# The joint stages between the scans of a state-space network: how outputs and inputs are handed out, and three buffers for the tiles of the outputs

## The chip, the cores and the metric

The kernel runs on one core of one Trainium2 chip. The metric is the device time of one execution in microseconds, as the median of the runs shown. The profile is that of one execution of the same kernel.

## The reference

A batch of four images of 64 x 64 pixels with 96 channels goes through four residual layers. Layers 0 and 1 are state-space blocks, layers 2 and 3 are an attention without softmax and a feed-forward layer with rounded operands. What matters here are the first two layers. Cut to its steps, with shapes left out, one of them is:

```
x   = x + block(groupnorm(x))               # 32 groups of 3 channels, over the whole image
block(x):
  xz      = x @ in_proj_w.T                 # 96 -> 2 * 192 channels: xp and the gate z
  xc      = silu(depthwise_conv3x3(xp))
  for four directions k (rows, columns, both reversed):
      dt, B, C = split(x_proj[k] @ xc_k)    # 6 + 16 + 16 rows
      delta    = softplus(dt_proj[k] @ dt + bias)
      h[l]     = exp(delta[l] * A) * h[l-1] + delta[l] * u[l] * B[l]    # 16 states a channel
      y_k[l]   = sum over states of h[l] * C[l], + D * u[l]
  y       = sum of the four y_k, each turned back to rows
  y       = layernorm(y) * silu(z)          # over the 192 channels of a pixel
  return y @ out_proj_w.T                   # 192 -> 96 channels
```

The recurrence over the 4096 pixels of an image is the scan.

## The kernel before, in words

**Units.** A pair of images is worked on together, so each of the two state-space layers has two units, and there are four units in all: layer 0 pair 0, layer 0 pair 1, layer 1 pair 0, layer 1 pair 1. Each unit has three steps. `scan_inputs` (L157) makes the inputs of the scan: it normalises and projects the image (`xn`, `ips`), writes the gate to HBM (`zs` to `zg`), and computes the convolution, in part as nine matmuls with diagonal weights (`conv_product`, L189, `cps`) and in part as chains of nine VectorE instructions (`conv_chain`, L203 and L205, into `u`). At its end it begins the projection and discretisation for the first piece of the scan (`scan.begin`: `xps`, `btps`, `bpps`, `dps`, `delta`, `du`, and the transposes `dups` with their copies `dut`, L478 and L480). `PairScan.scan` runs the scan itself. `scan_outputs` (L272) makes the outputs from the sums `y`, which the scan has stored in HBM.

**The outputs.** `scan_outputs` takes 256 pixels of both images at a time, 16 groups in all. A group loads the gate (`zt`, L285), the residual (`xr`, L287) and the sums (`ys`, three loads on L296); VectorE takes the statistics (`ystats`, `ymv`); POOL takes a power for the reciprocal deviation (`ln_rs`, L81); ScalarE normalises `ys` (L311); TensorE turns it in six transposes (`pt`, L319), ScalarE scales these into `gt` (L321), VectorE multiplies `gt` with `zt` (L328), TensorE projects (`po`, L335 in layer 0; L345, L346 and L348 in layer 1), and the sum with the residual (`xo`) is stored. In layer 0 VectorE also takes the statistics for the group norm of the next layer, and after the sixteenth group the norm is finished (`mv`, `gm`, `gv`, L123 to L138). These tiles live in the pool `c2`, which has two buffers of each, and three in the last unit.

**Stages.** The program has nine stretches in a row: inputs of unit 0; scan 0; joint stage; scan 1; joint stage; scan 2; joint stage; scan 3; and the token layers, which contain the outputs of unit 3. In a joint stage the outputs of the unit that has just been scanned and the inputs of the next unit are traced together. Both are generators. `scan_outputs` yields after every group, so 16 times; `scan_inputs` yields 20 times (eight projections of each image, a yield after every second, then six rounds of two yields). `between_scans` (L142) takes one group of the outputs and then two pieces of the inputs, in turn, so that the inputs are used up after ten groups.

**What sets the order.** Outside the scans the order of each engine is not that of the program text alone: a scheduler places each instruction on its engine's list when its operands and a buffer are there by its own estimate, with the order of tracing as priority. Within the scan every instruction is kept in program order. On the chip each engine then takes its list strictly in order. All loads and stores are issued by one queue, SP, also in order. The pools of a joint stage (inputs `a`, `a2`, `a_ps`; outputs `c2`, `c_ps`) are given back when both generators are done, and the scan's pools take that memory.

Of the kernel before, what the change touches and what calls it, by code (L numbers as in the profile page):

```python
# [141 lines left out]
def between_scans(tc, cst, ident, half, pn, u, before, scan, after):  # L142


    with ExitStack() as stage:
        ins = scan_inputs(tc, stage, cst, ident, half, pn, u, scan, *after)
        if before is not None:
            pp = stage.enter_context(tc.tile_pool(name="c_ps", bufs=2, space=PSUM))
            outs = scan_outputs(tc, stage, cst, ident, half, pn, *before, pp)
            for _ in outs:  # L150
                for _ in range(2):
                    next(ins, None)
        for _ in ins:
            pass
# [117 lines left out]
def scan_outputs(tc, stage, cst, ident, half, pn, layer, pr, pp, turned="pt", summed="po"):  # L272

    nc = tc.nc
    par, zg, x_src, x_dst, y = layer.par, layer.zg[pr], layer.x_src, layer.x_dst, layer.y[pr]
    p2 = stage.enter_context(tc.tile_pool(name="c2", bufs=3 if layer.last and pr else 2))
    if not layer.last:
        norms = [GroupNorm(p2, pn, f"gn{2 * pr + i}", NT // 2) for i in range(2)]
    wo = p2.tile([128, 3, C], F32, name="wo", bufs=1)
# [2 lines left out]
    for g in range(NT // 2):  # L282
# [46 lines left out]
        bufs = 1 if summed == "po" else None  # L329
# [559 lines left out]
def token_layers(tc, cst, ident, half, x, outputs, a):  # L889
# [3 lines left out]
    with ExitStack() as stage:  # L893
# [28 lines left out]


        outs = scan_outputs(tc, stage, cst, ident, half, None, *outputs, pp, "mm", "o")
        images = [image(b) for b in range(NB)]
        begun, going, turns = 0, [], 0
# [13 lines left out]
def hybrid_kernel(ctx: ExitStack, tc: tile.TileContext, a):  # L940
# [14 lines left out]
    with ExitStack() as scans:  # L955
        pw = scans.enter_context(tc.tile_pool(name="s_w", bufs=1))
        pn = scans.enter_context(tc.tile_pool(name="s_n", bufs=1))
        units = []
        for n in range(2):
            layer = ScanLayer(tc, pw, dram, x, {k: a[f"l{n}_{k}"] for k in ("par", "wi", "wx", "wdt", "wo")}, n)  # L960
            units += [(layer, pr) for pr in range(NB // 2)]
            x = layer.x_dst
        units[0][0].after = units[2][0]
        with ExitStack() as scanning:
            pk = scanning.enter_context(tc.tile_pool(name="s_k", bufs=2))
            pu = scanning.enter_context(tc.tile_pool(name="s_u", bufs=1))
            pq = scanning.enter_context(tc.tile_pool(name="s_q", bufs=1))
            pd = scanning.enter_context(tc.tile_pool(name="s_d", bufs=2, space=DRAM))
            cst["sel"] = pu.tile([NP, NS, 256], BF16, name="sel")
            nc.sync.dma_start(out=cst["sel"], in_=a["c_sel"])  # L970
            cst["ident16"] = pu.tile([128, 128], BF16, name="ident16")
            nc.vector.tensor_copy(cst["ident16"], ident)
            u = [pu.tile([128, L], F32, name=f"u{j}") for j in range(3)]
            before = None
            for unit in units:
                scan = PairScan(tc, pk, pq, pd, cst, ident, u, *unit)
                between_scans(tc, cst, ident, half, pn, u, before, scan, unit)
                scan.run()
                before = unit
        token_layers(tc, cst, ident, half, x, before, a)  # L980
# [113 lines left out]
```

## Time and profile before

| | us |
|---|---|
| median of 3 runs (10634.33 to 10654.25) | 10643.59 |
| the profiled execution | 10644.94 |
| its span, first to last instruction | 10643.2 |
| inputs of unit 0, up to the first `bp` of scan 0 | 0 to 154.9 |
| first joint stage, end of the last `ysum` to the first `bp` | 2461.7 to 2678.6 |
| second joint stage | 4984.3 to 5197.6 |
| third joint stage | 7500.1 to 7713.7 |
| token layers with the outputs of unit 3 | 10014.9 to 10643.2 |

In the profile PE is TensorE's matmul and PEld its weight load, DVE is VectorE, ACT ScalarE, POOL GpSimd and SP the engine that issues the transfers. A slice of the page is one fortieth of the span, 266 us, and a digit is the busy share in tenths. In a list of groups the columns are line, engine, operation and tile, shapes, count, busy time, mean duration in ns, and the idle time just before with what ended it. A matmul of float32 operands shows as two records.

### The profile page before, as it was taken

What the parts mean: (1) busy time and instruction counts of PE and PEld (TensorE: products, weight loads), DVE (VectorE), ACT (ScalarE), POOL (GpSimd) and SP (SyncE); (2) the same over time, 40 slices, a digit from 0 to 9 for tenths busy, and PEclk for the clock granted to TensorE, in tenths of its full rate; (3) what the DMA queues carried; (4) which work ended last, traced back from release to release, by engine and by line L of the source; (5) the groups of instructions that cost most, each with busy time, mean ns of one, the idle gap of its engine ahead of it and who ended that gap; (6) DMA issues with size and microseconds to landing.
All of it is one profiled execution on the core that took longest, in us unless ns stands there. A gap on an engine that the chain in (4) does not pass through costs nothing. (4 is left out here: it accounts for less than half of the span.)

```text
span 10643.2 us, 142480 instructions
## 1 busy us (share of the span) xinstructions
PE 8055.8 (76%) x47648; PEld 5971.9 (56%) x47648; DVE 9608.1 (90%) x6922; ACT 8760.2 (82%) x18779; POOL 9008.7 (85%) x5298
## 2 busy tenths in 40 slices
PE   7777777777777777777877777777777777777666
PEld 4555555554555555555455555555455555555554
DVE  8999999997899999998899999999699999999755
ACT  6888888885888888887688888888598888888666
POOL 3999999993899999997499999999299999999745
PEclk9888899988888898988888988998888889899877
DMA  4677777775667777777467777777566777777710
GB/s 154 208 211 215 216 222 218 219 213 158 196 210 216 217 220 220 219 214 210 149 209 211 220 219 218 220 219 217 143 209 211 213 220 219 220 217 219 199 35 25
DMA packets 905175, 2120.41 MB, mean 199 GB/s; under 512 B 330583, under 2 KB 640153, under 8 KB 706713
## 3 DMA queue, kind: packets, MB, share of 16 engines
q1 hardware_dynamic: 904440, 2111.30, 68.3%
q8 instruction: 378, 6.19, 0.2%
q14 instruction: 357, 2.92, 0.1%
HBM read 1949.56 MB, written 161.48 MB: 198 GB/s over the span
## 5 line engine op out<-in xcount | busy, mean ns | idle before, releaser
L71 POOL TENSOR_TENSOR h<-h,cb 128x1024 f32<-128x1024 f32 x3072 | 7191.2, 2364 | 234.4 <-issue 58.6
L71 DVE TENSOR_TENSOR_SCAN h<-da,last,bp 128x1024 f32<-128x1024 f32 x2064 | 4736.8, 2335 | 147.1 <-PE bp L71 23.8
L71 ACT ACTIVATE x<-dut,bt 128x128 f32<-128x128 f32 x12288 | 3494.8, 370 | 1.5 <-PE bp L71 1.1
L71 PE MATMUL yp<-ident,h 128*128 128x128 f32 x24576 | 3370.2, 297 | 9.8 <-POOL h L71 9.8
L71 PEld LDWEIGHTS yp<-ident,h 128*128 128x128 f32 x24576 | 3197.1, 157 | 125.7 <-issue 75.5
L71 ACT ACTIVATE da<-delta,amat 128x1024 f32<-128x1024 f32 x2752 | 3060.2, 1138 | 96.0 <-DVE h L71 94.9
L71 PE MATMUL bp<-ident,x 128*128 128x128 f32 x10240 | 1679.2, 316 | 1282.1 <-DVE h L71 923.7
L71 PEld LDWEIGHTS bp<-ident,x 128*128 128x128 f32 x10240 | 1362.6, 162 | 1840.7 <-ACT x L71 1026.7
L71 DVE TENSOR_TENSOR bp<-du,bp 128x1024 f32<-128x1024 f32 x1472 | 1780.1, 1213 | 266.0 <-PE bp L71 264.4
L71 DVE TENSOR_TENSOR_SCAN h<-da,bp 128x1024 f32<-128x1024 f32 x688 | 1537.7, 2274 | 52.7 <-ACT da L71 11.4
L71 PE MATMUL bp<-bparts,sel 96*128 96x512 bf16 x2944 | 918.8, 398 | 760.4 <-DVE h L71 741.2
L71 PEld LDWEIGHTS <-sel 96*128 96x128 bf16 x2944 | 226.8, 100 | 1554.8 <-DVE h L71 1043.7
L71 ACT ACTIVATE bp<-delta,amat 128x1024 f32<-128x1024 f32 x320 | 358.1, 1119 | 528.3 <-DVE h L71 526.3
L71 POOL TENSOR_TENSOR dbu<-du,bb 128x1024 f32<-128x1024 f32 x320 | 754.6, 2358 | 0.0
L71 DVE TENSOR_TENSOR_SCAN h<-bp,last,dbu 128x1024 f32<-128x1024 f32 x240 | 558.9, 2329 | 10.4 <-POOL dbu L71 7.1
L81 POOL TENSOR_TENSOR ln_rs<-ln_ve,half 128x4 f32<-128x4 f32 x64 | 82.4, 1288 | 567.2 <-DVE ln_ve L79 442.0
L71 PE MATMUL xps<-u,wx 128*76 128x512 f32 x720 | 532.0, 824 | 0.0
L71 ACT ACT_TABLE_LOAD x380 | 487.5, 1283 | 34.6 <-DVE gn_norm L138 22.4
L71 POOL COPY last<-h 128x2 f32<-128x2 f32 x1152 | 215.8, 187 | 351.0 <-DVE h L71 349.1
L71 POOL TENSOR_TENSOR du<-delta,u 128x1024 f32<-128x1024 f32 x188 | 496.2, 2639 | 0.0
L71 ACT COPY ysum<-yp 128x1024 f32<-128x1024 f32 x192 | 194.4, 1012 | 300.3 <-PE yp L71 300.3
L71 PE MATMUL dps<-cdt,wdt 12*128 12x512 f32 x752 | 435.0, 658 | 0.0
(159 smaller groups left out, 6328.0 us busy)
## 6 DMA issues: line engine op xcount, KB each, us to landing
cb<-crow SPq DMA_DIRECT2D x1024, 1024.0 KB
cb<-crow SPq DMA_DIRECT2D x1024, 512.0 KB
bb<-crow SPq DMA_DIRECT2D x384, 256.0 KB
bb<-crow SPq DMA_DIRECT2D x128, 512.0 KB
y<-ysum SPq DMA_DIRECT2D x192, 256.0 KB
kept<-y SPq DMA_DIRECT2D x160, 256.0 KB
y<-ysum SPq DMA_DIRECT2D x64, 512.0 KB
zt<-zg SPq DMA_DIRECT2D x64, 384.0 KB
```

Of the source, the lines that this page charges most:

```text
L71: return self.tc.keep_in_program_order(getattr(self.engine, op)(*args, **kwargs))
L81: nc.gpsimd.tensor_tensor(rs, ve, half, ALU.pow)
```

## The change

Two lines differ. In `between_scans` the outputs are counted, and after a group one piece of the inputs is taken, after every fourth group two, so that 20 pieces go to 16 groups: five pieces for four groups. In `scan_outputs` the pool `c2` has three buffers of each tile in every unit.

```diff
@@ between_scans @@
             outs = scan_outputs(tc, stage, cst, ident, half, pn, *before, pp)
-            for _ in outs:
-                for _ in range(2):
+            for g, _ in enumerate(outs):
+                for _ in range(2 if g % 4 == 3 else 1):
                     next(ins, None)
         for _ in ins:
             pass
@@ scan_outputs @@
-    p2 = stage.enter_context(tc.tile_pool(name="c2", bufs=3 if layer.last and pr else 2))
+    p2 = stage.enter_context(tc.tile_pool(name="c2", bufs=3))
```

## The prediction

> **What bounds the kernel now.** I read the page's busy rows and slices first, then the busy time by window around the places where the slices dip, then groups, waits and the order of time inside one dip.
>
> ```profile
> PE 8055.8 (76%) x47648; PEld 5971.9 (56%) x47648; DVE 9608.1 (90%) x6922; ACT 8760.2 (82%) x18779; POOL 9008.7 (85%) x5298
> ...
> DVE  8999999997899999998899999999699999999755
> ...
> POOL 3999999993899999997499999999299999999745
> ```
>
> Over the span DVE and POOL are the full engines, but the slices show two regimes. The four scans run DVE and POOL at 9; POOL falls to 2 to 4 between them, in the three joint stages. The change touches no instruction of a scan, so the 90% of DVE says nothing on it: only the dips count. Each dip by windows, cut at three places: from the end of the last sum of a scan to PE's first work, to the end of the last instruction of the inputs (the copy of `dut`, L480), to the first `bp` matmul of the next scan (columns: stretch and length, busy time and count of PE, weight loads, DVE, ACT and POOL, granted clock, DMA share, GB/s).
>
> ```profile
> 2461.70:2476.80 15.10, 0.00 (x0) 0.00 (x0) 2.66 (x12) 0.58 (x3) 7.51 (x22) 0.59 0.82 190
> 2476.80:2632.10 155.30, 144.03 (x426) 70.01 (x426) 130.39 (x240) 95.08 (x181) 17.27 (x11) 0.97 0.48 140
> 2632.10:2678.60 46.50, 28.48 (x86) 17.73 (x87) 23.11 (x77) 17.47 (x40) 4.57 (x5) 0.68 0.38 110
> 4984.30:4999.30 15.00, 0.73 (x3) 0.47 (x3) 3.27 (x13) 1.33 (x4) 7.51 (x22) 0.59 0.83 206
> 4999.30:5153.60 154.30, 143.34 (x425) 69.59 (x423) 129.62 (x238) 94.44 (x180) 17.27 (x11) 0.97 0.47 139
> 5153.60:5197.60 44.00, 26.33 (x86) 16.36 (x87) 23.20 (x77) 17.50 (x40) 4.57 (x5) 0.74 0.40 117
> 7500.10:7515.00 14.90, 0.00 (x0) 0.00 (x0) 2.52 (x12) 0.47 (x2) 7.52 (x22) 0.59 0.83 198
> 7515.00:7667.80 152.80, 146.28 (x546) 77.41 (x546) 118.11 (x210) 99.56 (x192) 16.58 (x11) 0.98 0.48 141
> 7667.80:7713.70 45.90, 31.20 (x150) 27.14 (x151) 13.04 (x46) 19.82 (x46) 4.03 (x4) 0.63 0.37 108
> ```
>
> The joint stages last 216.9, 213.3 and 213.6 us. In their middle PE is busy 93% (144.0/155.3), 93% and 96%: PE bounds it, with DVE at 84, 84 and 77%. In the tails, 46.5 + 44.0 + 45.9 = 136.4 us together, no engine is over 68%: six groups of outputs are left over and run alone, one waiting for the other:
>
> ```profile
> POOL ln_rs L81 <- DVE ln_ve L79: 21.1, 3, 10.9
> ...
> DVE xo L337 <- PE po L335: 13.1, 5, 3.7
> PEld po L335 <- DVE gt L328: 10.3, 4, 2.8
> ...
> ACT ys L311 <- DVE shift L307: 9.8, 4, 3.9
> ```
>
> These waits of the first tail run in a ring: DVE waits for PE, PE for DVE, ACT for DVE. That the next scan waits for the ring's end is seen in order of time:
>
> ```profile
> 2673.02 0.68 DVE L337 TENSOR_TENSOR xo<-xr,po 96x512 f32<-96x512 f32 x1 [3.74 <-PE po L335]
> ...
> 2674.41 1.01 DVE L123 BATCH_NORM_AGGREGATE mv<-gn_stats 96x2 f32<-96x96 f32 x2
> ...
> 2678.62 1.01 PE L71 MATMUL bp<-bparts,sel 96*128 96x512 bf16 x2 [0.24 <-DVE gn_ve L79]
> ```
>
> The pools of the scan take the memory that the stage's pools give back, so its first `bp` comes only when outputs, norms and inputs are all done. The tail is on the path of the whole kernel.
>
> **What the Trainium skill says.** "Perfetto Trace Analysis", Optimization Strategy: where the most-contended engine changes over time, interleaving the regimes can help, and the same gap repeating may mean too few buffers. The windows agree with the first half (PE at 93%, then 61%); the second fits the tail, whose groups come every 6 to 8 us with two buffers. "TensorE: Matmul & The Clock Gate", What's actually happening: the array falls to half clock after an idle window and returns after about 3.4 us of sustained work. The trace agrees in direction: granted clock 0.97 in the first middle and 0.68 in its tail, and `po` matmuls of 396 ns mean against 611. "ScalarE: Activation LUTs", What ACT_TABLE_LOAD costs: about 1283 ns a load; the trace's 380 loads have a mean of 1283. The built program has as many loads after the change as before, so I price them at nothing; ACT is busy only 61% of the middle, which would hide a few.
>
> **The change part by part.** No computing instruction is added or removed. In the order of the built program the scans, the first stage and the last one stand as before; in each joint stage the number of `po` groups behind the last transposes of the inputs (`dups`, L478) falls from six to none.
>
> *Six groups into the middle, by PE.* Warm, ten `po` groups take 20.2 us (80 records), 2.02 each, and 66 `pt` transposes, eleven groups, 11.5 us, 1.05 each. The first tail holds six groups of `po` and five of `pt`: 6 x 2.02 + 5 x 1.05 = 17.4 us of warm PE time (cold, the tail's rows show 20.9 + 6.9 us). The second is alike. For the third, the middle has 146.3 us of PE for the same ten groups against 144.0, so 0.23 more a group: 18.8 us. If PE stays at the share of each middle, and 1.9 us of it (one product of the inputs, below) moves ahead:
> first (144.0 + 17.4 - 1.9)/0.927 = 172.0, 16.7 longer than 155.3;
> second (143.3 + 17.4 - 1.9)/0.929 = 170.9, 16.6 longer;
> third (146.3 + 18.8 - 1.9)/0.957 = 170.5, 17.7 longer.
>
> *The same by DVE.* The first tail's 23.1 us less some 2.2 for the group norms make 20.9; with 130.4 that is 151.3 us, at the middle's 84% 180.2, so 24.9 longer. Second: (129.6 + 21.0)/0.84 = 179.3, 25.0 longer. Third, without norms: (118.1 + 13.0)/0.773 = 169.6, 16.8 longer, so PE's 17.7 decides there.
>
> *What still stands behind.* In the first two stages the norms, 5.6 us from the `xo` of 2673.02 to `bp`; some conv matmuls and `dups` now stand between the last `po` and the norms' matmuls, so 5 behind PE's end (bounds 4 and 8). The third has no norms: 2 us for the copies of `dut` and `xo` (bounds 1 and 4).
>
> *Sum.* By PE: (46.5 - 16.7 - 5) + (44.0 - 16.6 - 5) + (45.9 - 17.7 - 2) = 24.8 + 22.4 + 26.2 = 73 us. By DVE: 16.6 + 14.0 + 26.2 = 57 us. Both engines cannot wait less for each other while both do more, so I take the slower reading rounded, **58 us**.
>
> *Third buffer.* It adds a third set of `zt`, `xr`, `ys`, `gt` and `xo` (13 KB a partition). With 16 groups in some 172 us, 11 us apart, loads are early anyway; in the first middle DVE waited 2.6 us for `ys`. I take 0; bounds are 0 and 2.6 us a stage. Its price is on SP: a third group's five loads, at about 0.4 us of issue each 2 us, now come before the stage's fourth `xn`. PE's first products use the three `xn` loaded earlier, which hides them; uncovered, it is 2 us a stage.
>
> *`xn` loads.* In the built program the first three move ahead of the store of the last `ysum` on SP, and the first product ahead of the first `pt`: hence the 1.9 us (two cold `ips` records at 2477.97 take 1.92). These loads wait for a DVE and an ACT instruction; the last scan on DVE ended at 2456.9, before SP needs to store `ysum` at 2461.7, so I charge nothing. Queued behind them are two weight loads and that store, for which the outputs wait. Bounds: 3 us gained a stage, 3 lost.
>
> **Rivals.** *(a) In-order stalls, slower.* PE and DVE take their work in a fixed order, so a `pt` or `po` that isn't ready holds back the conv matmuls behind it. In the first middle this cost PE about 8.5 us for ten groups (7.4 for `gt`, 1.1 for `ys` after the lead-in), 0.85 a group. The gain of the PE reading, 24.8 us over 16 groups, is gone at 1.5 us more a group, 2.4 in all; the tail itself shows 9.1 + 3.3 = 12.4 us over six, 2.1. At 3.0 a stage loses 16 x 0.65 = 10 us: 10674 us. Against it: in the new order other matmuls stand between a group's `pt` and its `po`, as in the middle of before. *(b) Only the buffer works.* If the merged middle stretches by all that the tail gives, but groups then come as in the last stage, which has three buffers already (16 groups in 10066 to 10155, 5.9 us each) instead of 6.6, 6.2 and 7.6, then 5 x (0.7 + 0.2 + 1.7) = 13 us: 10630. *(c) The start of the scan is late for another reason,* since `delta`, `du` and `dups` of the inputs now share engines with outputs: six groups' DVE time, 21 us, put before `du` would leave 46 - 21 - 5 = 20 us a stage, 10584, which is my forecast again. *(d) That outputs and inputs don't end together* is ruled out by the built order.
>
> **How the numbers follow.** The profiled execution took 10644.9 us (span 10643.2 and 1.7 around it), 1.3 above the median of 10643.6; I count from the median: 10643.6 - 58 = **10586 us**. Chances: absorbed in the middle 0.85 (own range 10562 to 10612: the PE reading and 10 more, down to 32); (b) or most of the gain eaten 0.10; (a) 0.05. A measurement of this kernel tells about 0.2%, 21 us, from no change. Of the first case I put nearly all beyond that: faster 0.86, same 0.09, slower 0.05. The range, 10560 to 10628, adds the bounds of the start and the norms and part of (b).
>
> **What would show it.** The stages should be 190 to 202 us long, no `po` should come after `dups`, POOL's dip should be narrower, and the granted clock should stay above 0.9 up to the norms. PE's wait for `gt` and `ys` over 25 us a stage would mean (a); a middle stretched to 195 us with DVE under 80% too. A changed length of a scan would be outside all of this, and prove the whole sum wrong.

## The result, and the profile after

| | before | after |
|---|---|---|
| median of 6 runs each, us | 10644.94 (10634.33 to 10654.25) | 10595.13 (10584.92 to 10607.82) |
| the profiled execution | 10644.94 | 10593.83 |
| joint stages (end of the last `ysum` to the first `bp`) | 216.9, 213.3, 213.6 | 197.2, 200.1, 195.1 |
| sum of the three | 643.8 | 592.4 |

The ratio of after to before is 0.9954, with a 95% interval of 0.9943 to 0.9966: 49.8 us less by the medians, where 58 were forecast. The three stages give 19.7, 13.2 and 18.5 us, 51.4 together, close to the 51.1 us by which the two profiled executions differ. So the gain is that of these stages; the rest of the program cancels to within half a microsecond.

The page after, the busy engines and two rows of slices:

```profile
PE 8027.2 (76%) x47648; PEld 5946.6 (56%) x47648; DVE 9610.8 (91%) x6922; ACT 8761.4 (83%) x18779; POOL 9023.9 (85%) x5298
...
DVE  8999999998999999998899999999799999999755
...
POOL 3999999993999999997599999999399999999645
```

The busy sums are those of before to within 29 us (PE has 28.6 less, 16 of them in the joint stages); the instructions are as many. DVE's dips between the scans have gone from 7, 8 and 6 to 8, 8 and 7, POOL's from 3, 4 and 2 to 3, 5 and 3. The slices can show no more than that: one is 265 us, longer than a stage.

The windows after, cut at the same events: PE's first work, the end of the copy of `dut`, the first `bp` (columns: stretch and length, busy time and count of PE, weight loads, DVE, ACT and POOL, granted clock, DMA share, GB/s). In the third stage `bp` comes 0.1 us after that copy, so there is no third window:

```profile
2454.80:2469.00 14.20, 0.00 (x0) 0.00 (x0) 1.84 (x9) 0.00 (x0) 7.16 (x22) 0.50 0.79 180
2469.00:2649.90 180.90, 164.31 (x507) 83.02 (x507) 151.15 (x309) 112.95 (x221) 25.31 (x16) 0.95 0.51 147
2649.90:2652.00 2.10, 0.78 (x7) 0.61 (x8) 0.96 (x7) 0.00 (x0) 0.55 (x2) 1.00 0.00 0
4955.60:4970.00 14.40, 1.43 (x2) 0.50 (x2) 1.94 (x10) 0.29 (x2) 7.54 (x22) 0.50 0.83 194
4970.00:5153.60 183.60, 167.11 (x506) 83.59 (x505) 151.14 (x308) 112.82 (x221) 25.23 (x15) 0.93 0.50 143
5153.60:5155.70 2.10, 0.78 (x7) 0.61 (x8) 0.95 (x7) 0.00 (x0) 0.55 (x1) 1.00 0.00 0
7462.40:7477.00 14.60, 0.14 (x1) 0.14 (x1) 2.75 (x12) 0.74 (x2) 7.54 (x22) 0.50 0.83 197
7477.00:7657.40 180.40, 169.72 (x696) 95.68 (x697) 129.96 (x256) 119.14 (x236) 20.39 (x15) 0.95 0.54 149
```

The tails of 44.0 to 46.5 us at a clock of 0.63 to 0.74 are gone. The middles are 25 to 30 us longer, at a clock of 0.93 to 0.95, and PE's share of them is 91, 91 and 94%. The share of a whole middle hides what happens in it. Two pieces of the first stage:

```profile
2569.00:2589.00 20.00, 18.07 (x48) 8.52 (x47) 19.88 (x26) 4.99 (x8) 0.00 (x0) 0.91 0.17 46
2629.00:2652.00 23.00, 20.98 (x78) 11.25 (x77) 9.88 (x25) 10.88 (x20) 0.55 (x2) 1.00 0.12 32
```

Half way, DVE is full (19.9 of 20 us). At the end PE is (21.0 of 23), and DVE is at 9.9. The bound passes from one to the other inside the stage.

PE's waits in the first middle (line that waits, line waited for, us, times, longest):

```profile
PE ips L227 <- DMA zt<-zg: 15.3, 1, 15.3
PE po L335 <- DVE gt L328: 7.0, 6, 1.9
PE ips L227 <- DVE ymv L304: 4.7, 1, 4.7
PE ips L227 <- ACT ys L311: 2.6, 1, 2.6
PE pt L319 <- ACT ys L311: 1.3, 2, 1.1
```

The first of them is the lead-in. For sixteen groups PE waits 7.0 us for `gt` and 1.3 for `ys`, against 7.4 and 1.1 for ten groups before. The `po` are spread, and a gate is ready when its turn comes. The order of time at the stage's end:

```profile
2644.78 0.68 DVE L337 TENSOR_TENSOR xo<-xr,po 96x512 f32<-96x512 f32 x1 [1.34 <-PE po L335]
...
2648.01 1.04 PE L478 MATMUL dups<-ident,du 128*128 128x128 f32 x8
...
2651.98 0.61 PE L71 MATMUL bp<-bparts,sel 96*128 96x512 bf16 x2 [0.25 <-DVE gn_ve L79]
```

The last `xo` stands ahead of the inputs' last transposes (`dups`). The norms (DVE's 0.96 us in the window of 2.10) end this stage and the second; in the third `bp` waits for the copy of `dut`.

### The profile page after: what moved, and what is told of

The parts are those of the page before. It is cut to its first block, busy times and chain, and to the rows that moved or that the text cites. A ratio compares the mean times of both kernels' runs of the same rounds, so it can differ in the third digit from the quotient of the medians.

```text
span 10592.1 us, 142441 instructions
## 1 busy us (share of the span) xinstructions
PE 8027.2 (76%) x47648; PEld 5946.6 (56%) x47648; DVE 9610.8 (91%) x6922; ACT 8761.4 (83%) x18779; POOL 9023.9 (85%) x5298
## 5 line engine op out<-in xcount | busy, mean ns | idle before, releaser
L71 DVE TENSOR_TENSOR_SCAN h<-bp,last,dbu 128x1024 f32<-128x1024 f32 x240 | 558.9, 2329 | 16.9 <-POOL dbu L71 15.9
L71 ACT COPY ysum<-yp 128x1024 f32<-128x1024 f32 x192 | 194.5, 1013 | 287.1 <-PE yp L71 287.1
```

The lines of the kernel that those rows point to most:

```text
L71: return self.tc.keep_in_program_order(getattr(self.engine, op)(*args, **kwargs))
```

## The experiments

Each ratio is to runs of the kernel before on the same chip. Three chips were used for e1 to e9, for e10 to e12 and for e13; the kernel before had medians of 10643.6 to 10647.5 us on them. e5 and e6 have one run each. A stage's length is from one profiled execution of each kernel. In these profiles each of the four scans, whose code no kernel changes, took 2296 to 2320 us, and a median moves with them; so the stages' own lengths tell more than the medians. Two stretches show how far a length moves by itself. The inputs of unit 0, which nine of these kernels run with the same instructions in the same order, took 153.3 to 158.5 us. The outputs of unit 3, the same in twelve, took 135.5 to 142.1 us from the end of the last `ysum` to the last `xo`. So a difference of up to some 6 us in one stage is read only where stages or kernels agree on it. "Sum" is against 643.8 us.

| kernel | stages, us | sum | median, us | ratio to before (95%) |
|---|---|---|---|---|
| after | 197.2, 200.1, 195.1 | -51.4 | 10595.13 | 0.9954 (0.9943 to 0.9966) |
| e1 order only | 203.8, 203.5, 199.0 | -37.5 | 10607.51 | 0.9965 (0.9951 to 0.9980) |
| e2 buffer only | 202.0, 198.6, 208.2 | -35.0 | 10609.97 | 0.9966 (0.9954 to 0.9978) |
| e12 third buffer of the loads only | 208.5, 205.3, 209.4 | -20.6 | 10617.02 | 0.9972 (0.9963 to 0.9980) |
| e3 three pieces for two groups | 197.8, 198.3, 197.0 | -50.7 | 10601.45 | 0.9962 (0.9948 to 0.9977) |
| e4 one piece for one group | 194.5, 193.9, 201.6 | -53.8 | 10581.97 | 0.9942 (0.9928 to 0.9957) |
| e5 less DVE | 189.7, 191.3, 199.1 | -63.7 | 10556.78 (one run) | |
| e6 less PE | 185.7, 186.9, 174.4 | -96.8 | 10521.07 (one run) | |
| e7 `shift` on POOL | 228.0, 228.7, 218.2 | +31.1 | 10692.63 | 1.0049 (1.0033 to 1.0066) |
| e9 `shift` and the gate on POOL | 246.8, 246.8, 230.4 | +80.2 | 10750.5 | 1.0106 (1.0091 to 1.0121) |
| e10 a chain for two products | 195.3, 199.2, 194.4 | -54.9 | 10576.53 | 0.9939 (0.9924 to 0.9954) |
| e11 e10 with e4 | 196.0, 193.3, 191.3 | -63.2 | 10586.42 | 0.9940 (0.9922 to 0.9958) |
| e13 half a chain, with e4 | 190.5, 189.4, 195.8 | -68.1 | 10568.19 | 0.9927 (0.9913 to 0.9941) |

### Each half alone: e1 and e2

e1 is the kernel after with `bufs=3 if layer.last and pr else 2`; e2 is the kernel before with `bufs=3`.

> The new handing out alone: five pieces of the inputs to four groups, with two buffers in the first three units as before. Theory A (the gain comes from the six groups that leave the tail): the three joint stages are within 4 us each of those of the changed kernel (197.2, 200.1, 195.1), and the time is 43 to 55 us under before. Rival B (with two buffers a group's loads come too late once groups share the engines with inputs): each stage is 6 us or more longer than that, and half the gain or more is gone, 10615 us or above.

> The third buffer alone: two pieces of the inputs after every group as before, so that six groups run alone at the end. Theory A: the ring of waits between DVE, PE, ACT and POOL sets the pace of the six, not the loads, so 0 to 8 us under before, no difference that can be measured. Rival (b) of the prediction: the groups come every 5.9 us as in the last stage, 13 us under before. Rival B: over 21 us under before.

Measured: the order alone takes 37.5 us off the stages, the buffer alone 35.0. Together they take 51.4 and not 72.5. e1 met neither of its theories: its stages are 6.6, 3.4 and 3.9 us longer than those of after. Every expectation of a small buffer was wrong, that of the prediction first of all; e2's rival B, over 21 us, was met. What three buffers do in the old order, first stage, cut at the end of the inputs:

```profile
2461.20:2625.30 164.10, 143.41 (x426) 70.89 (x426) 133.50 (x258) 97.14 (x186) 26.12 (x34) 0.94 0.53 152
2625.30:2663.20 37.90, 24.05 (x87) 15.27 (x88) 21.42 (x67) 15.56 (x37) 3.59 (x5) 0.76 0.38 110
```

Before, lead-in and middle were 170.4 us together and the tail 46.5. Now they are 164.1 and 37.9: 6.3 us come from the middle and 8.6 from the tail. In the other two stages the tail gives 7.3 and 8.5 us, and the middle 7.4 less and 3.1 more, so the tails give 24.4 of the 35.0. In the tail the first four sums with the residual now come in a close run:

```profile
2633.45 0.68 DVE L337 TENSOR_TENSOR xo<-xr,po 96x512 f32<-96x512 f32 x1 [0.50 <-PE po L335]
...
2636.34 0.68 DVE L337 TENSOR_TENSOR xo<-xr,po 96x512 f32<-96x512 f32 x1
...
2639.35 0.68 DVE L337 TENSOR_TENSOR xo<-xr,po 96x512 f32<-96x512 f32 x1
...
2643.12 0.67 DVE L337 TENSOR_TENSOR xo<-xr,po 96x512 f32<-96x512 f32 x1
```

These three gaps are 2.9, 3.0 and 3.8 us, where they were 4.5, 5.8 and 9.2 before; the prediction's "every 6 to 8 us" holds for the mean of 6.6. The last two, 7.9 and 6.7 us, are no shorter than before (6.7 and 6.8): when only two groups are left, the ring is back. The tail's waits say the same:

```profile
DVE xo L337 <- PE po L335: 7.6, 3, 3.7
DVE ystats L303 <- DMA ys<-y: 5.7, 1, 5.7
```

The first of them was 13.1 us in five waits. The second, for the loads themselves, hardly changed:

```profile
DVE ystats L303 <- DMA ys<-y: 6.6, 2, 5.8
```

So the gain of this tail isn't that DVE waits less for loads. The reading that fits is that with a third group in flight the ring of waits has other work to turn on. The two halves don't add up because both shorten the same tail: the order by emptying it, the buffer by running it faster. On top of the new order the buffer still takes 6.6, 3.4 and 3.9 us, 13.9 together, which is near the 10.6 that it takes outside the tails in the old one.

### Which tiles need the third buffer: e12

```diff
-        zt = p2.tile([128, 3, 256], F32, name="zt")
+        zt = p2.tile([128, 3, 256], F32, name="zt", bufs=3)
```

The same is done for `xr` and `ys`, on the kernel before; `gt`, `xo` and the small tiles keep two.

> The kernel before with three buffers for zt, xr and ys alone, the tiles that are loaded; gt, xo and the small ones stay at two, and the handing out is that of before. Three buffers for all of them gave joint stages of 202.0, 198.7 and 208.1 us against 216.9, 213.3 and 213.6, 35 us. If the loads' lead is what counts, each stage is within 3 us of the former. If it is a third group in flight on the engines (gt and xo, and the order that the scheduler then finds), within 3 us of the latter; if both, between them.

20.6 of the 35.0 us come with the three tiles of the loads, so more than half; the first two stages lie between the two theories. The tail of the first stage is 38.6 us (37.9 in e2), but lead-in and middle are 169.9 (164.1). The three stages agree: the tails are 22.0 us shorter than before (24.4 in e2), the rest 1.4 longer (10.6 shorter in e2). So the third buffer of the loads serves the tails, that of the others the middles of the first two. Which of the others, and how much of it is the order that the scheduler makes with them, was not separated.

### How exact the handing must be: e3 and e4

```diff
-                for _ in range(2 if g % 4 == 3 else 1):
+                for _ in range(2 if g % 2 else 1):      # e3
+                for _ in range(1):                      # e4
```

> Three pieces of the inputs to two groups, three buffers: in the built order two or three groups stand behind the inputs instead of six or none. Theory A (each group that leaves the tail saves the difference of its time alone, some 6.8 us, and its time inside the middle, some 3 to 4 us): 28 to 38 us under before, between the two kernels. Rival C (what counts is that the scan's first inputs and the norms are ready together; a tail of two groups is hidden): as fast as the changed kernel within 8 us.

> One piece of the inputs after every group, so that the outputs are done first and the last four pieces of the inputs run alone, with the group norms beside them; three buffers. Theory PE (a joint stage is as long as PE's work, wherever it stands): the norms are hidden and the conv matmuls fill the end, stages 2 to 6 us shorter than in the changed kernel, 52 to 68 us under before. Theory DVE (VectorE's chains and the outputs' small instructions set the pace of the middle): the last chain and the chain from dps to dut stand alone at the end, each stage 3 to 12 us longer than in the changed kernel, 15 to 42 us under before.

e3 leaves three groups of outputs behind the inputs and its stages are as long as those of after (593.1 against 592.4), as its rival C had it: with three buffers a short tail is cheap. e4 lets the outputs end first. Its first two stages gain 2.7 and 6.2 us more, as theory PE had it, and the third loses 6.5; each is about what a stage moves by itself. The end of its first stage:

```profile
2630.00:2655.30 25.30, 24.00 (x83) 11.72 (x82) 12.75 (x26) 10.46 (x16) 1.09 (x2) 1.00 0.09 21
```

PE is busy for 24.0 of 25.3 us at full clock, and DVE for half of it: what is left at the end is convolution on PE. The last `xo` comes 16.9 us ahead of `bp` here, 7.2 in the kernel after. So that outputs and inputs end at the same time is not what matters. By this reading what matters is that nothing is left whose steps wait for each other. Whether the third stage lengthened by more than chance, and why, is open.

### Which engine bounds the merged stage: e5 and e6

```diff
-        for tap in range(9):      # in conv_chain
+        for tap in range(7):      # e5
-        for tap in range(9):      # in conv_product
+        for tap in range(6):      # e6
```

> The changed kernel with two of the nine taps left out of each of the eight convolution chains on VectorE, so part of the convolution isn't computed: 16 instructions of 1.27 us, 20 us less of DVE in each joint stage, PE as before. If PE alone bounds a joint stage, each is 0 to 5 us shorter than 197, 200 and 195 us. If DVE bounds it, 13 to 20 us shorter. If the two bound different parts of it one after the other, 6 to 12 us here and about as much in the kernel with less PE work.

> The changed kernel with three of the nine taps left out of each of the eight convolution products on PE, so part of the convolution isn't computed: 24 matmuls of 0.89 us, 21 us less of PE in each joint stage, DVE as before. If PE bounds a joint stage, each is 14 to 21 us shorter than 197, 200 and 195 us. If DVE does, 0 to 6 us shorter. If each bounds a part, 6 to 14 us.

Both leave out a part of the convolution: e5 two of nine steps of every chain on DVE, e6 three of nine matmuls of every product on PE. The whole stages, first and third, of e5 and then of e6:

```profile
2459.20:2648.90 189.70, 161.84 (x512) 80.90 (x512) 136.21 (x309) 112.36 (x222) 29.41 (x38) 0.94 0.56 153
...
7435.70:7634.80 199.10, 169.71 (x696) 96.49 (x697) 114.77 (x251) 119.77 (x238) 26.01 (x37) 0.91 0.55 150
```

```profile
2440.00:2625.70 185.70, 147.54 (x464) 75.42 (x464) 153.73 (x325) 112.67 (x222) 30.39 (x38) 0.89 0.56 157
...
7416.80:7591.20 174.40, 148.42 (x649) 85.53 (x650) 131.85 (x267) 119.05 (x237) 28.75 (x37) 0.91 0.62 169
```

In the first stage 17.7 us less of DVE (154.0 to 136.2) bring 7.5, and 17.6 less of PE (165.1 to 147.5) bring 11.5; the second stage has 8.8 and 13.2. Each of them bounds a part of the stage, as the two pieces above show. In the third stage 21.4 us less of PE bring 20.7, and 17.9 less of DVE bring nothing (4.0 longer, within what a stage moves by itself): there it is PE alone.

### Work moved to the idle engine: e7 and e9

POOL is busy for 33 of the first stage's 197 us. `shift` is the small product between `ln_rs` and the normalisation of `ys`.

```diff
-        nc.vector.scalar_tensor_tensor(shift, mv[:, :, :, 0], -1.0, rs, ALU.mult, ALU.mult)
+        nc.gpsimd.tensor_tensor(shift, mv[:, :, :, 0], rs, ALU.mult)
+        nc.gpsimd.tensor_scalar(shift, shift, -1.0, None, ALU.mult)
```

e9 moves the product `gt` with `zt` (L328) to POOL as well.

> The changed kernel with the small product that makes shift out of ln_rs (L307) moved from DVE to POOL, as two instructions there. In the changed kernel DVE waits about 0.9 us for POOL at this product in most groups, 12.6 us in the first joint stage. If DVE's waits count, as the theory of DVE in the middle says, each joint stage is 4 to 10 us shorter, 62 to 80 us under before. If PE bounds, or the scheduler's order gives the waits another place, the stages are within 3 us of 197, 200 and 195.

> As the kernel with shift on POOL, and the product of gt with zt (L328, 16 of 0.95 us on DVE in a stage) on POOL too, where 768 elements should take some 1.8 us by the rows of POOL with 1024 elements in 2.36. If DVE bounds the middle, each joint stage is 10 to 20 us shorter than in the changed kernel. If the longer way through POOL delays po, on which PE waits already, or PE bounds, within 4 us of the kernel with shift on POOL, or longer.

Neither theory of e7 was met: its stages are 31 us longer than before and 82 longer than after. e9 is another 49 us longer, which its second theory had allowed for. Where the time is, is seen in the group of `ln_rs`, which was not changed (POOL's groups of the first stage: busy, mean ns | idle before; after, then e7):

```profile
L81 POOL TENSOR_TENSOR ln_rs<-ln_ve,half 128x4 f32<-128x4 f32 x16 | 26.0, 1624 | 136.1 <-DVE ln_ve L79 126.6 <-ACT zs L233 9.5
```

```profile
L81 POOL TENSOR_TENSOR ln_rs<-ln_ve,half 128x4 f32<-128x4 f32 x16 | 54.0, 3372 | 124.1 <-DVE ln_ve L79 124.1
```

A power of 128 x 4 numbers takes 3.4 us in the mean instead of 1.6. One of e7's in order of time, with what DVE does meanwhile:

```profile
2539.81 5.69 POOL L81 TENSOR_TENSOR ln_rs<-ln_ve,half 128x4 f32<-128x4 f32 x1 [14.95 <-DVE ln_ve L79]
```

```profile
2539.74 4.86 DVE L205 SCALAR_TENSOR_TENSOR u<-img,par,u 128x1024 f32<-128x1024 f32 x4
```

The power lasts until 0.9 us after four steps of a chain that run on DVE without a gap. The longest, and its chain:

```profile
2586.01 17.48 POOL L81 TENSOR_TENSOR ln_rs<-ln_ve,half 128x4 f32<-128x4 f32 x1 [4.95 <-DVE ln_ve L79]
```

```profile
2585.78 16.82 DVE L205 SCALAR_TENSOR_TENSOR u<-img,par,u 128x1024 f32<-128x1024 f32 x14
```

Again it ends 0.9 us after the chain. In the kernel after DVE itself takes `shift`, and so waits for each power, at most 1.2 us:

```profile
DVE shift L307 <- POOL ln_rs L81: 12.6, 15, 1.2
```

The wait looked like waste and was a shelter: in the first stage DVE stopped after at most two instructions with two SBUF inputs, and POOL's power then ran at its own pace. Without it the power is held up, and ACT waits for `shift`:

```profile
ACT ys L312 <- POOL shift L308: 70.3, 11, 19.6
```

In the kernel after ACT waited 38.5 us for DVE's `shift`. The 31.8 us more are about what this stage is longer (30.8). That the chain holds the power is what the traces show and what the Trainium skill states ("SBUF — State Buffer", SBUF: two separate sides: VectorE and GpSimd share a pair of ports as an exclusive lock, and the loser is blocked; a VectorE instruction with two SBUF inputs takes it against a GpSimd instruction that reads SBUF). The trace agrees, with 1.0 us undisturbed and up to 17.5 us in e7. It can be counted over the whole of three kernels, before, after and e7. Of their 192 powers 117 took at most 1.1 us, and none of these began while VectorE ran an instruction with two SBUF inputs (a step of a chain, `gt` with `zt`, or `du`). 70 took more than 1.5 us; 69 of these began so, and 68 ended 0.85 to 0.95 us after the end of such an instruction. No run took the chain away, but little room is left for another cause.

### Work moved from PE to DVE: e10, e11 and e13

```diff
-        conv_product(*((1, 8 * n) if n < 6 else (0, 8 * n)))
+        if n < 6:
+            conv_product(1, 8 * n)
+        elif n == 6:
+            conv_chain(0, 48)
```

This is e10: two products of PE (nine matmuls of 512 columns each) become one chain of nine instructions on DVE. e11 adds the handing of e4. e13 has the handing of e4, leaves the first of the two products on PE, and makes the second a chain of half the rows, `conv_chain(0, 56, 8)`.

> The changed kernel with the last two convolution products of PE (image 0, rows 48 to 63, 18 matmuls of 0.89 us) computed as one chain on DVE (0.8 + 8 x 1.27 = 10.9 us) in every stage of inputs. Taking 21 us from PE shortened the joint stages by 11.5, 13.1 and 20.7 us, taking 20 us from DVE by 7.5, 8.8 and -4.0. If the two bounds can be traded against each other at those rates: 16 us less PE is worth 8.8, 10.0 and 15.8, 11 us more DVE costs 4.1, 4.8 and 0, so stages 5, 5 and 16 us shorter than in the changed kernel and the inputs of unit 0 some 8 us shorter, 75 to 95 us under before. If the chain on DVE at the end delays the start of the scan, its 11 us stand there: as fast as the changed kernel or slower.

> The same chain in place of two products, with one piece of the inputs after every group, so that outputs end first. In the kernel without the chain this handing out made the first two joint stages 3 and 6 us shorter than five pieces to four groups and the third 6.5 longer. If the same holds, within 8 us of the kernel with the chain and five pieces to four groups. If a stage whose end has only inputs is then held by two chains of DVE in a row, the stages are 5 to 12 us longer than there.

> One piece of the inputs after every group, and one of the two products moved to DVE instead of both: image 0, rows 56 to 63, as a chain of half the length (some 6 us of DVE by 9 instructions of about 0.7 us for 8 us of PE). In the last 25 us of a joint stage PE was busy 24.0 and DVE 12.8 with both products on PE, PE 13.1 and DVE 24.6 with both on DVE. If the end is held by whichever engine has more there, the halves come to some 19 us on each, so each stage is 3 to 6 us shorter than 194.4, 193.9 and 201.6 or 196.0, 193.3 and 191.3, 70 to 85 us under before. If the end is a chain of waits rather than work, the stages stay within 3 us of the better of the two, 55 to 66 us under before.

e10 gains 1.9, 0.9 and 0.7 us a stage, no more than chance and far less than the trade would give. PE's load went down, but the new chain is one of the last three to be traced, and DVE is full at the end. In e10 two groups of outputs come after `dups` again and share DVE with the chain. In e11 the outputs are done, but the steps of the norms wait between those of the chains: from `mv` to `bp` the first stage takes 10.8 us (5.8 in the kernel after). e11's stages are 0.7 longer, 5.9 and 3.1 shorter than e10's, within the 8 us of its first theory; its third stage didn't lengthen as that of e4 did. e10 in 23 us that end 1.1 us before its first stage does, and e11 in its last 25.5:

```profile
2629.00:2652.00 23.00, 11.34 (x49) 7.55 (x47) 19.94 (x39) 9.65 (x17) 2.43 (x2) 0.86 0.15 43
```

```profile
2640.00:2665.50 25.50, 13.11 (x55) 8.04 (x53) 24.55 (x38) 10.02 (x16) 1.59 (x1) 0.77 0.06 16
```

At the end the kernel after had PE at 20.98 and DVE at 9.88 of 23 us. The bound has only changed hands. e13 leaves both with work until the end, and its first stage is balanced:

```profile
2452.80:2643.30 190.50, 156.31 (x495) 78.28 (x496) 158.77 (x335) 112.33 (x222) 29.89 (x39) 0.92 0.55 154
```

PE and DVE have 156 and 159 of 190.5 us. Its stages are 4.0, 4.5 and 5.8 us shorter than those of e4, as expected, and the inputs of unit 0 gain as well (150.4 us; 153.3 to 158.5 with both products on PE). At 10568.19 us it has the lowest median of the full versions here, 78 us under before. Its interval (to 0.9941) reaches into those of e4, e10 and e11, so the medians don't rank these four. The stages put it ahead of e4 three times out of three; against e11 it is ahead in two, by 4.9 us in the sum, which is not enough.

## Why the prediction was right, and where it was off

**The tail is on the path of the whole kernel: right.** 51.4 us off the stages are 51.1 off the profiled execution and 49.8 off the medians.

**The slower of the two readings: right as a choice.** The sums against what the middles measured:

| middle | by PE | by DVE | measured |
|---|---|---|---|
| first | 172.0 | 180.2 | 180.9 |
| second | 170.9 | 179.3 | some 185 (PE begins 1.4 us ahead of the cut) |
| third | 170.5 | 169.6 | 180.4 |

DVE's terms were met in the first stage: 151.3 us of work foreseen, 151.15 found; a share of 84% taken over, 83.6% found. But "by DVE" was half a reason. e5 and e6 show that neither engine bounds the first two stages through and through. And with the work that PE turned out to have there (164.3 us, not 159.5) PE's own reading of the first stage is 164.3/0.927 = 177.2 us, so that DVE's sum came closest doesn't show DVE to be the bound; that part is luck. Why the shares of the old middles carried over so well was not tested.

**The third middle: the mis-sized term.** The sum had (146.3 + 18.8 - 1.9)/0.957 = 163.2/0.957. PE's work was 169.7 us, 6.5 more, which at 0.957 is 6.8 us; its share was 0.941, worth another 3.1. Together that is the 9.9 us between 170.5 and 180.4. The 1.9 us of lead came to 0.1 here (PE's 0.14 us in the lead-in), and PE's inputs (`ips`) took longer: 664 ns a record against 613. In the first stage PE also had 164.3 us instead of 159.5, but there PE's reading wasn't the one taken.

**The lead: half or less.** PE's first work came 14.2 us after the last `ysum`, not 15.1: 0.9 us instead of 1.9, and 0.6 and 0.3 by the cuts of the other two.

**Behind the inputs' end: too dear.** 5, 5 and 2 us were foreseen, 2.1, 2.1 and 0.1 measured. The norms' chain begins while PE still works on the inputs' last matmuls, so only its end is left over.

These three partly cancel. The net of the stages was 16.6, 14.0 and 26.2 foreseen, and 19.7, 13.2 and 18.5 measured: the third fell 7.7 us short, the first gave 3.1 more.

**The third buffer: the step that failed.** It was priced at 0, with 2.6 us a stage as the upper bound, from DVE's wait for `ys` in the middle. It is worth 35.0 us alone and 13.9 on top of the order. The reading looked for its worth at one wait in the middle. But 24.4 of the 35.0 us came from the tails, where the ring of waits, which the prediction itself showed, has only two groups to turn on. Rival (b) did price the tail, by the last stage's 5.9 us a group, and got 13 us where 35 were measured: in the first tail three gaps of five went down to some 3 us, and the middles of the first two stages gave time too. The total still came out near because the order alone gave 37.5 where the sum had given it 58. That part of the closeness is luck.

**Rivals.** (a) is out: PE's waits for `gt` and `ys` are 8.3 us in the first stage, and the waits of `ips` behind DVE and ACT 7.3, against the 25 that would have meant it. (c) was a third way to 58 us; in the first two stages the norms end the stage and not the chain of the inputs. In the third the inputs do end it: `bp` waits 0.87 us for the copy of `dut`, behind PE's last products. The chances had the right order, but that one of the two edits alone would bring 35 us was in none of the cases.

**Signs.** Stages of 190 to 202 us, no `po` after `dups`, a clock above 0.9 up to the norms: all seen, and POOL's dips are shallower by at most a tenth. That a changed length of a scan would "prove the whole sum wrong" was too strict a test. Scan 0 took 5.3 us less, scan 1 2.0 less, scan 2 4.2 more and scan 3 2.7 more with the same instructions; together with the inputs of unit 0 (1.6 less) and the token layers (2.5 more) that is 0.5 us. The same scans differ by as much between the other kernels.

**Open.** Whether the third stage really lengthens when DVE has less to do (e5, 4.0 us) or the outputs come first (e4, 6.5 us) was not settled: both are about what a stretch with unchanged order moves by itself (5.2 and 6.6 us), and the scheduler makes another order in each. Nor was it told apart how much of the third buffer's worth is room on the chip and how much is the other order that it lets the scheduler make.

## What to carry to other kernels

When the last groups of a stage run alone with no engine full (none over 68% here) and the waits form a ring, there are two remedies, other work beside them or one more group in flight; each shortens the same tail, so their gains need not add (37.5 and 35.0 us alone, 51.4 together here), and each should be measured alone. Price a merged stage by both engines' work over the share that they reached in the mixed stretch, take the longer, and then read the result in short pieces: the bound can pass from one engine to the other inside the stage, and then work moved from one to the other may only move the bound (e10). A short wait of a busy engine for an otherwise idle one may be what lets the idle one finish, so moving work "to the idle engine" is tried before it is believed.

## What the runs showed of the hardware

- In these traces a small GpSimd instruction is held while VectorE runs instructions with two SBUF inputs, and VectorE isn't slowed by it: in e7 the chain's steps had a median of 1.273 us beside a power and of 1.276 without one. The power `ln_rs` (128 x 4, float32) took 1.0 us in the median of the whole kernel before. In e7's first stage, where VectorE no longer waits for it, its sixteen instances had a median of 1.9 us and a maximum of 17.5:

```profile
L81 POOL TENSOR_TENSOR ln_rs<-ln_ve,half x16: 1037/1934/17481, 2476.0 to 2667.0; 128x4 f32<-128x4 f32 x16
```

- For an elementwise product of 128 x 768 numbers GpSimd took 1.81 us (median of e9's `gt`) and VectorE 0.96 (median after). e9's stages are 49 us longer than e7's over 48 groups, about 1 us a group. That this is near the difference between the two doesn't show it to be the cause; e9's powers also lasted longer, up to 22.6 us.
